# Edge values as three bf16 parts: a graph layer with its edge sums moved to bf16 matmuls

## The chip, the cores and the metric

The kernel runs on one core of a Trainium2 chip. A core has a matrix engine (TensorE, PE in the profile; PEld are its weight loads), a vector engine (VectorE, DVE), an engine for activation functions (ScalarE, ACT), GpSimd (POOL), which here issues the indirect DMAs, and SyncE (SP), which here issues nearly all other DMAs. Each engine works through its own instructions in the order in which the kernel gives them, and waits for another engine or a DMA where an instruction needs it. Matmuls write to PSUM, which this kernel divides into six banks named "mm" and two named "seg"; everything else lies in SBUF or in DRAM.

The metric is device time in microseconds, median over the runs of the kernel.

## The reference

One layer of a graph network on 6250 nodes of 256 features, with 106250 edges of 64 features. In short:

```python
xn = layernorm(x)
sums = segment_sum(edge_attr, src, n)                 # this is what the change touches
agg  = sums / maximum(segment_sum(ones, src, n), 1.0)
gnn  = relu(concat(xn, agg, u) @ W1 + b1) @ W2 + b2
mix  = 4 layers of: h = layernorm(x); x += linear_attention(h)
                    h = layernorm(x); x += gelu(h @ W1 + b1) @ W2 + b2
x = x + gnn + mix(xn)
x = x + relu(relu(z @ We1[e] + be1[e]) @ We2[e] + be2[e])   # z = layernorm(x), e = argmax(z @ router)
```

All is in fp32. The edge sums don't depend on the layers of `mix`; they are needed only after the last attention.

## The kernel before, in words

The nodes are worked on in 13 groups of 512 (the last has 106). X, the running sum of all nodes, stays in SBUF for the whole kernel. There are no queues that a planner fills: the order of the instructions is the order of the Python code, which is written out by hand (`manual_schedule`), and each engine keeps it.

**Layer 0's first half.** A loop over the groups normalizes x (`norms_a`, `norms_b`), transposes it (`norm1_t`), makes k and q of layer 0 (`qk`), transposes them (`context_t`) and adds to the attention's context (`context`).

**The layer loop.** For l = 0, 1, 2 and each group g, one iteration does the feed-forward part of layer l for group g and the attention's first half of layer l+1 for it: `ff_in` (eight outputs of 512 columns, each into an mm bank, L209, with a GELU on ACT to `hid`, L212), `attn_out_t` (transposes), `context_t(g-1)`, `ff_out` (L223), `norm1(g)`, `context(g-1)` (L499), `attn_out(g+2)` (L184), `norm1_t`, `qk` (L419 for k, L453 for q) and at its end `norm2(g+2)`. `norm2` takes statistics on DVE (L119, L120), a square root on ACT (L121, tile sd) and normalizes on DVE (L127). What `norm2` makes is used by `attn_out_t` of the next iteration; its square root stands on ACT ahead of the next iteration's GELUs.

**The edge work** is spread through both. An edge is a lane of one of 831 tiles of 128 edges; a batch is four tiles, and there are 208 batches. For a tile, a 128x128 matrix eq is 1 where two edges of the tile have the same source; eq times the tile's edge rows gives each edge the sum over all edges of the tile with its source. One edge per source then adds its row to a table in DRAM (`tabs`); the others are sent to a dump row, which the last of the 66 columns, a falling weight, decides. The steps of a batch:

- `edge_load`: two DMAs on SP, the edge values (128x4x64, fp32) and `all`, the sources of the batch, repeated on all 128 partitions (int32)
- `edge_match`: on DVE, eq from `all` and `srcf`, the sources as fp32, one per partition (L352)
- `edge_sum`: on PE, four fp32 matmuls of 66 columns into a seg bank (L365; each takes two passes in the profile), and a copy to `s` on ACT (L367)
- `edge_add`: on DVE the row numbers (L379, L381), then four indirect DMAs that add in DRAM (L383, POOL)

`edges(n)` does n times: an add, a sum, a load and a match, each of another batch; loads and matches run ahead of the sums, the adds one batch behind. In the layer loop `share` says how often each of the four calls of an iteration does this: (2, 1, 1, 2) in most iterations of l = 0 and 1. The calls stand after `ff_in`, after `norm1`, after `norm1_t` and after `qk`; the last stands just ahead of `norm2`.

**The rest** (from about 2100 us) is the last layer, the graph network's own part, the router and the experts; no edge work is in it but the reading of the tables.

## Time and profile before

| | |
|---|---|
| median of 3 runs | 2975.72 us (2973.36 to 2979.73) |
| the profiled execution: time, span | 2972.65 us, 2970.9 us |
| busy: PE, PEld, DVE | 2849.9, 2056.6, 1536.1 us |
| busy: ACT, POOL | 1126.9, 1458.1 us |
| mean granted clock of PE | 0.976 |
| layer 0's first half | about 40 to 205 us |
| layer loop, l = 0, 1, 2 | about 205 to 830, 840 to 1480, 1480 to 2100 us |

The profile gives for each engine its busy time, and a chain of waits, followed back from the last instruction, whose shares say which engine was waited for last. A group of instructions stands under its line, its engine and its tiles ("seg<-edge,eq"), with how many there are, their busy time in us, the mean duration in ns and the idle time of the engine just before them. The timeline lists instructions by start and duration in us, like ones in a row together, with the idle time before them in brackets and what ended it. In the windows view a line is a stretch: its length, then busy us (and instructions) of PE, PEld, DVE, ACT and POOL, the granted clock of PE, the DMA engines' share and GB/s.

### The profile page before, as it was taken

The page shows a single profiled execution, that of the slowest core. Times are in us where ns is not written, and L with a number is a line of the kernel's source. Part 1 is how long each engine was busy: PE and PEld are TensorE (multiplying, and loading weights), DVE is VectorE, ACT ScalarE, POOL GpSimd, SP SyncE. Part 2 cuts the span into 40 slices and gives each one's busy share as a digit, 9 for nine tenths or more (in the row PEclk, how much of TensorE's full clock was granted, in tenths as well). Part 3 has the DMA queues.
Part 4 walks back from the last instruction along what each step waited for, and adds up shares of the span by engine and source line. Part 5 has one row for each costly group of instructions (what it writes and reads, how often), then busy time and mean ns, then how long its engine had stood idle before and what let it go on. Part 6 is the DMA issues. An engine that isn't in the chain of part 4 may idle for free.

```text
span 2970.9 us, 36212 instructions
## 1 busy us (share of the span) xinstructions
PE 2849.9 (96%) x12594; PEld 2056.6 (69%) x12594; DVE 1536.1 (52%) x4194; ACT 1126.9 (38%) x1995; POOL 1458.1 (49%) x1108
## 2 busy tenths in 40 slices
PE   7989999999989999999899999999799999999977
PEld 5767777777766777777767777777566766765654
DVE  7874645555546464646455555544343543543453
ACT  6754343434334344343443434344223223223232
POOL 0445777777747777777746656454001001001057
PEclk9999999999989999999999999999899999999888
DMA  8234555655555555555734443231200101102152
GB/s 257 35 50 84 75 96 75 97 73 97 79 110 82 89 82 88 78 94 78 133 59 79 76 75 49 42 43 18 74 15 29 36 22 29 36 22 72 55 188 76
DMA packets 368983, 219.12 MB, mean 74 GB/s; under 512 B 265913, under 2 KB 333469, under 8 KB 368792
## 3 DMA queue, kind: packets, MB, share of 16 engines
q1 hardware_dynamic: 241832, 175.32, 22.9%
q0 software_dynamic: 126144, 40.61, 17.3%
q8 instruction: 102, 1.67, 0.2%
q14 instruction: 89, 0.73, 0.1%
q10 hardware_dynamic: 816, 0.79, 0.1%
HBM read 135.46 MB, written 85.49 MB: 74 GB/s over the span
## 4 chain that ended last, share of the span: by engine, by line
PE 87%; DVE 7%; ACT 2%; issue 2%; POOL 1%; DMA 1%; POOLq 0%; SPq 0%; ACTq 0%; DVEq 0%
PE mm L223 23%; PE mm L209 23%; PE seg L365 5%; PE mm L184 5%; PE mm L419 5%; PE mm L499 4%; PE mm L453 4%; PE mm L699 3%; PE mm L135 3%; PE mm L715 3%; PE mm L700 2%; PE mm L487 1%; PE mm L479 1%; POOL out_x L987 1%; PE mm L972 1%
## 5 line engine op out<-in xcount | busy, mean ns | idle before, releaser
L383 POOL DMA_INDIRECT tab<-s,row x831 | 1313.5, 1581 | 738.4 <-issue 352.8
L209 PE MATMUL mm<-hT,w 128*128 128x512 f32 (+1 forms) x1664 | 686.5, 570 | 5.8 <-ACT hid L212 4.0
L223 PE MATMUL mm<-w,hid 128*128 128x256 f32 (+1 forms) x3136 | 687.8, 380 | 0.0
L223 PEld LDWEIGHTS mm<-w,hid 128*128 128x128 f32 (+1 forms) x3136 | 592.5, 190 | 80.1
L209 PEld LDWEIGHTS mm<-hT,w 128*128 128x128 f32 x1664 | 301.3, 190 | 354.7 <-issue 321.9
L121 ACT ACTIVATE sd<-mv,eps 128x4 f32<-128x4 f32 (+1 forms) x117 | 34.8, 297 | 991.3 <-DVE mv L120 991.1
L225 DVE TENSOR_TENSOR X<-mm,X 128x512 f32<-128x512 f32 (+1 forms) x100 | 68.1, 681 | 632.1 <-PE mm L223 632.1
L775 POOL DMA_INDIRECT xtab<-rows,to x49 | 48.2, 984 | 643.1 <-DVE to L773 574.1
L212 ACT ACTIVATE hid<-mm,col 128x512 f32<-128x512 f32 (+1 forms) x416 | 249.1, 669 | 101.1 <-PE mm L209 98.8
L365 PEld LDWEIGHTS seg<-edge,eq 128*128 128x128 f32 x1662 | 207.2, 192 | 21.5 <-issue 17.2
L365 PE MATMUL seg<-edge,eq 128*128 128x66 f32 x1662 | 202.7, 270 | 0.0
L139 ACT ACTIVATE hT<-mm,col 128x512 f32<-128x512 f32 (+1 forms) x208 | 145.0, 748 | 142.1 <-PE mm L135 140.8
L184 PE MATMUL mm<-M,qT 128*128 128x256 f32 (+1 forms) x784 | 191.3, 400 | 2.3 <-DVE M L539 2.3
L419 PE MATMUL mm<-hT,wqkv 128*128 128x512 f32 (+1 forms) x416 | 183.5, 584 | 3.5 <-ACT hT L139 3.5
L499 PE MATMUL mm<-z,kt 128*128 128x256 f32 (+1 forms) x784 | 181.8, 385 | 0.2 <-ACT kt L481 0.2
L453 PE MATMUL mm<-wqkv,hT 128*128 128x256 f32 (+1 forms) x784 | 177.7, 379 | 0.0
L453 PEld LDWEIGHTS mm<-wqkv,hT 128*128 128x128 f32 (+1 forms) x784 | 148.4, 190 | 40.7 <-issue 22.5
L184 PEld LDWEIGHTS mm<-M,qT 128*128 128x128 f32 (+1 forms) x784 | 156.2, 201 | 27.4 <-DVE M L539 4.2
L499 PEld LDWEIGHTS mm<-z,kt 128*128 128x128 f32 (+1 forms) x784 | 147.4, 192 | 19.1 <-ACT kt L481 0.4
L135 PE MATMUL mm<-ident,z 128*128 128x128 f32 x882 | 124.8, 277 | 28.3 <-DVE z L127 16.9
L352 DVE TENSOR_TENSOR eq<-all,srcf 128x512 f32<-128x512 int32 x208 | 142.9, 687 | 3.1 <-DMA all<-in_srct 2.7
L379 DVE TENSOR_SCALAR a<-s,twice,dump 128x4 f32<-128x4 f32 x208 | 60.4, 291 | 154.4 <-ACT s L367 154.4
(209 smaller groups left out, 3310.5 us busy)
## 6 DMA issues: line engine op xcount, KB each, us to landing
all<-in_srct SPq DMA_DIRECT2D x207, 256.0 KB, 3.8
xtab<-zero SPq DMA_DIRECT2D x32, 1036.0 KB, 10.2
edge<-in_edge SPq DMA_DIRECT2D x207, 128.0 KB, 2.7
tab<-s,row POOLq DMA_INDIRECT x831, 3.3
xg<-xtab SPq DMA_DIRECT2D x32, 259.0 KB, 5.9
w<-in_w SPq DMA_DIRECT2D x8, 1024.0 KB, 13.8
tab<-zero SPq DMA_DIRECT2D x40, 162.5 KB, 4.9
tb<-tab SPq DMA_DIRECT2D x48, 130.0 KB, 4.1
```

The source lines that it names most:

```text
L135: nc.tensor.transpose(ps[:, j * P:j * P + r], z[j][:r, k * P:(k + 1) * P], ident[:r, :r])
L139: nc.scalar.activation(hT[:, k, :cnt], ps[:, :cnt], AF.Identity, bias=col[:, bcol + k:bcol + k + 1], scale=col[:, gcol + k:gcol + k + 1])
L184: nc.tensor.matmul(ps[:r, j, :], qT[:, k, c0:c0 + r], M[:, k, :], start=(k == 0), stop=(k == 1))
L209: nc.tensor.matmul(ps[:, :cnt], w[:, k, b * P:(b + 1) * P], h[:, k, :cnt], start=(k == 0), stop=(k == 1))
L212: nc.scalar.activation(hid[:, :cnt], ps[:, :cnt], AF.Gelu, bias=col[:, c:c + 1], scale=1.0)
L223: nc.tensor.matmul(ps[:r, j, :], hid[b][:, c0:c0 + r], w[:, b, :], start=(b == 0), stop=(b == NHB - 1))
L352: nc.vector.tensor_tensor(out=eq[:, :m], in0=ALL.pop(b)[:, :m], in1=srcf[:, t0:t0 + m].unsqueeze(2).to_broadcast([P, m, P]), op=ALU.is_equal)
L365: nc.tensor.matmul(ps[:, i, :], eq[:, i, :], e[:, i, :], start=True, stop=True)
L383: nc.gpsimd.indirect_dma_start(out=tabs[i], out_offset=bass.IndirectOffsetOnAxis(ap=row[:, i:i + 1], axis=0), in_=s[:, i, :DE + 1], in_off ...
L419: nc.tensor.matmul(ps[:, :cnt], w[:, k, c:c + P], h[:, k, :cnt], start=(k == 0), stop=(k == 1))
L453: nc.tensor.matmul(ps[:r, j * D:(j + 1) * D], h[:, k, (j0 + j) * P:(j0 + j) * P + r], w[:, k, :D], start=(k == 0), stop=(k == 1))
L499: nc.tensor.matmul(ps[:, b, :], kt[b][:r, j * P:(j + 1) * P], z[:r, j, :], start=(j == 0), stop=(j == n - 1))
```

## The change

Each edge value is split into three bf16 numbers whose sum is exactly the fp32 value: the upper half of its 32 bits is a bf16 by itself (`upper`, a view of the same memory that takes every second half-word), the rest is a subtraction on DVE, the upper half of the rest is the second part, and what is still left, another subtraction, is the third. eq becomes bf16, which holds 0 and 1 exactly. The sum of a tile is then three bf16 matmuls into the same PSUM columns in place of one in fp32. The new step `edge_split` makes the parts, as far ahead as `edge_match` makes eq.

The sources that `all` repeats are now 16 bits wide. They are loaded once into an unused part of qT (`wide`), cast on DVE (`half`), written to DRAM (`near`) and loaded from there.

The edge work of layer 0's first half is taken out: groups 2 to 12 there had one `edges()` each, and group 1 two matches. Now group 2 has the cast and the write to DRAM, group 10 two loads, group 11 two matches and splits and a load. `share` in the layer loop is (2, 1, 1, 2) also for the first four groups of l = 2, and (2, 1, 1, 1) for the later ones, where it was (2, 1, 1, 1) for the first six and (1, 1, 1, 1) then.

```diff
+    near = dram.tile([P, ET], I16, name="near")
...
+            wide = qT[:, 1, N - ET:].bitcast(I32)
+            half = qT[:, 1, N - 2 * ET:N - ET].bitcast(I16)[:, :ET]
+            nc.sync.dma_start(out=wide, in_=srct.rearrange("o (p t) -> (o p) t", p=P))
+            near_row = near.rearrange("(o p) t -> o (p t)", o=1)
...
-                al = ep.tile([P, CB * EB, P], I32, name="all", bufs=2)
+                al = ep.tile([P, CB * EB, P], I16, name="all", bufs=2)
                 nc.sync.dma_start(out=al[:, :m].rearrange("p m e -> p (m e)"),
-                                  in_=srct[:, t0 * P:(t0 + m) * P].to_broadcast([P, m * P]))
+                                  in_=near_row[:, t0 * P:(t0 + m) * P].to_broadcast([P, m * P]))
...
-                eq = ep.tile([P, EB, P], F32, name="eq", bufs=3)
+                eq = ep.tile([P, EB, P], BF16, name="eq", bufs=3)
...
+            def upper(t):
+                return t.bitcast(BF16).rearrange("p j (c h) -> p j c h", h=2)[:, :, :, 1]
+
+            def edge_split():
+                b = steps["split"]
+                if b >= steps["load"]:
+                    return
+                steps["split"] += 1
+                m = min(EB, ET - b * EB)
+                e = EDGE[b]
+                rest = ep.tile([P, EB, DE], F32, name="rest", bufs=3)
+                nc.vector.tensor_tensor(out=rest[:, :m], in0=e[:, :m, :DE], in1=upper(e[:, :m, :DE]), op=ALU.subtract)
+                low = ep.tile([P, EB, DE], BF16, name="low", bufs=3)
+                nc.vector.tensor_tensor(out=low[:, :m], in0=rest[:, :m], in1=upper(rest[:, :m]), op=ALU.subtract)
+                PART[b] = upper(rest), low
...
-                e = EDGE.pop(b)
+                e = upper(EDGE.pop(b))
+                mid, low = PART.pop(b)
...
-                    nc.tensor.matmul(ps[:, i, :], eq[:, i, :], e[:, i, :], start=True, stop=True)
+                    nc.tensor.matmul(ps[:, i, :], eq[:, i, :], e[:, i, :], start=True, stop=False, skip_group_check=True)
+                    nc.tensor.matmul(ps[:, i, :DE], eq[:, i, :], mid[:, i, :], start=False, stop=False, skip_group_check=True)
+                    nc.tensor.matmul(ps[:, i, :DE], eq[:, i, :], low[:, i, :], start=False, stop=True, skip_group_check=True)
...
                     edge_match()
+                    edge_split()
...
             norm1_t(0, 0)
-            edge_load()
-            edge_load()
             clear_tabs()
...
-                if g == 1:
+                if g == 2:
+                    nc.vector.tensor_copy(half, wide)
+                    nc.sync.dma_start(out=near, in_=half)
+                elif g == NG - 3:
+                    edge_load()
+                    edge_load()
+                elif g == NG - 2:
                     edge_match()
+                    edge_split()
                     edge_load()
                     edge_match()
-                elif g:
-                    edges()
+                    edge_split()
...
-                    share = ((1, 0, 0, 1) if g + 1 == NG else (2, 1, 1, 1) if g + 2 == NG or (l + 2 == DEPTH and g < 6)
-                             else (2, 1, 1, 2) if l + 2 < DEPTH else (1, 1, 1, 1))
+                    share = ((1, 0, 0, 1) if g + 1 == NG else (2, 1, 1, 1) if g + 2 == NG or (l + 2 == DEPTH and g > 3)
+                             else (2, 1, 1, 2))
```

More of the change, by code (lines that the diff above doesn't have):

```diff
@@ L12 @@
 I32 = mybir.dt.int32
+I16 = mybir.dt.int16
 BF16 = mybir.dt.bfloat16
@@ L321, in clear @@
                                   in_=zero[:, :XROW].unsqueeze(1).to_broadcast([P, XCLEAR // P, XROW]))
-            EDGE, ALL, EQ, SUM = {}, {}, {}, {}
-            steps = {"load": 0, "match": 0, "sum": 0, "add": 0}
+            EDGE, ALL, EQ, SUM, PART = {}, {}, {}, {}, {}
+            steps = {"load": 0, "match": 0, "split": 0, "sum": 0, "add": 0}
             def edge_load():
@@ L354, in edge_match @@
                 EQ[b] = (eq, m)
+            def upper(t):
[12 more added lines that the diff above has]
+                PART[b] = upper(rest), low
             def edge_sum():
                 b = steps["sum"]
-                if b >= steps["match"]:
+                if b >= min(steps["match"], steps["split"]):
                     return
```

## The prediction

> **What bounds it now.** I read the page first: busy shares, then the chain that ended last, then the costliest groups.

> ```profile
> PE 2849.9 (96%) x12594; PEld 2056.6 (69%) x12594; DVE 1536.1 (52%) x4194; ACT 1126.9 (38%) x1995; POOL 1458.1 (49%) x1108
> PE 87%; DVE 7%; ACT 2%; issue 2%; POOL 1%; DMA 1%; POOLq 0%; SPq 0%; ACTq 0%; DVEq 0%
> L365 PE MATMUL seg<-edge,eq 128*128 128x66 f32 x1662 | 202.7, 270 | 0.0
> L352 DVE TENSOR_TENSOR eq<-all,srcf 128x512 f32<-128x512 int32 x208 | 142.9, 687 | 3.1 <-DMA all<-in_srct 2.7
> ```

> PE sets the end, and the edge sums (L365) are on it, so their cost looks like gain. But the chain names only what came last; I asked next how near the second thing comes. The timeline of one steady iteration of the layer loop (six batches; 50.15 us from one L209 start to the next), PE:

> ```profile
> 465.89 1.90 PE L365 MATMUL seg<-edge,eq 128*128 128x66 f32 x16
> 467.63 13.96 PE L209 MATMUL mm<-hT,w 128*128 128x512 f32 x32
> 481.43 1.90 PE L365 MATMUL seg<-edge,eq 128*128 128x66 f32 x16
> 483.16 1.04 PE L135 MATMUL mm<-ident,z 128*128 128x128 f32 x8
> ```

> The same timeline, DVE and then ACT:

> ```profile
> 471.28 0.28 DVE L379 TENSOR_SCALAR a<-s,twice,dump 128x4 f32<-128x4 f32 x1
> 471.60 0.16 DVE L381 TENSOR_TENSOR row<-srcf,a 128x4 int32<-128x4 f32 x1
> 471.68 0.68 DVE L352 TENSOR_TENSOR eq<-all,srcf 128x512 f32<-128x512 int32 x1
> ...
> 473.29 0.42 DVE L119 BATCH_NORM_STATS2 st<-X 128x6 f32<-128x256 f32 x1
> ```

> ```profile
> 475.54 0.30 ACT L121 ACTIVATE sd<-mv,eps 128x4 f32<-128x4 f32 x1 [4.88 <-DVE mv L120]
> 475.85 1.28 ACT L212 ACT_TABLE_LOAD   x1
> 477.15 4.16 ACT L212 ACTIVATE hid<-mm,col 128x512 f32<-128x512 f32 x7
> ```

> The reader is to see one queue. At the iteration's end DVE does two batches of edge work (471.28 to 473.29, 1.0 us each), then norm2's statistics; ACT waits for these 4.88 us with sd, and the GELUs of the ff_in that PE began at 467.63 stand behind sd. ff_in makes eight outputs, but six banks ("mm") exist: output 7 needs the bank of GELU 1. PE gets to it at 467.63 + 10.35 = 477.98 (matmul 25 of 32 at 0.43 us); GELU 1 ends at 477.84. The cover is 0.15 us. So PE bounds this loop, with DVE and then ACT 0.15 us behind.

> [...] 512 elements take 0.69 us, 260 (L671) 0.43. [...] the new eq keeps fp32 srcf as an input, so I leave it at 0.69. [...] in the bf16 matmuls of the router (timeline, PE):

> ```profile
> 2228.91 0.25 PE L764 MATMUL mm<-oh,ones 128*128 128x96 bf16 x3
> 2229.01 0.25 PE L767 MATMUL mm<-oh,ones 128*128 128x32 bf16 x4
> 2229.12 0.68 PE L209 MATMUL mm<-hT,w 128*128 128x512 f32 x1
> ```

> Seven matmuls, each with its own weights, in 0.21 us. [...] stretches with the granted clock:

> ```profile
> 829.20:832.60 3.40, 1.99 (x14) 1.57 (x12) 2.06 (x9) 1.98 (x10) 2.70 (x2) 1.00 1.35 134
> 832.90:849.60 16.70, 12.28 (x33) 8.92 (x34) 5.24 (x14) 2.73 (x5) 12.39 (x8) 0.50 0.84 187
> ```

> The idle there before L487 was 2.27 us; one of 1.57 us (2073.96) brought no half clock.

> **The change, part by part.** *Sums on PE.* Before, a lone batch takes 251.10 to 251.94 = 0.84 us, a pair 465.89 to 467.63 = 1.74. After, 12 bf16 matmuls of 64 or 66 columns. Bounds for one: 25 ns (32 columns above) and 57 ns for the two that read every second half-word, were they paced like the fp32 pass (66/256 of the 216 ns of L223, and its 2 ns). I take 29, since 96, 64 and 32 columns together took 100 ns. The next fp32 weight load costs 0.11. Lone: 11 x 0.029 + 0.11 = 0.43; pair 0.79 (slow end 0.65 and 1.22). All 208 batches: 85 us of PE work gone.

> *Splits on DVE.* Two dependent subtractions of 256 elements: 0.43 + 0.04 to the dependent one (as L225 to L226, 0.73 for 0.69), then 0.34 to the next instruction (0.60 for 512): 0.81 us a batch, 168 us in all. An optimistic end is 0.4 (half), a pessimistic one 0.9.

> *The steady iteration.* From the end of ff_out to norm2, DVE now has four splits more (edges calls 2, 3, and two in 4). Two lie before qk's max, where DVE had 0.34 + 1.02 us of waits for PE: 1.62 minus these, and with PE there 0.7 earlier but DVE now last, leaves the second max 0.1 late. Two lie in the last call: +1.62 bare. So sd and GELU 1 are 1.7 late. PE meanwhile saves 0.7 before qk and 0.95 on the pair before ff_in, and waits for them: output 7 starts 0.155 after GELU 1 (as where GELU 1 was late, at 1255), an idle of 1.7 + 0.7 + 0.95 = 3.35 us. Of all PE savings only the pair after ff_in (0.95) is left on the path. Net 1.72 - 0.95 = +0.77 us.

> *The clock.* [...] mean +1.1 per iteration.

> *By layer.* Groups 0 to 10 are stalled: l=0 and l=1: 11 x 1.87; groups 11 and 12 have no norm2 behind them and keep PE's gain, 3.0: +17.6 each. l=2: four groups with six batches, 52.0 against 49.25 = +11.1; seven with one batch in the last call, idle 1.9, no half clock: 49.1 against 49.25 (two) and 48.4 (five): +3.2; last two groups -3.0: +11.3. Sum +46.5.

> *Layer 0's first half.* DVE bounds it (13.2 of 15 us busy): a, row, eq at 1.0 us leave groups 3 to 10: -8.0. In group 1 two eq and the wait for DMA all (1.6) go: -2.8. Group 2 gets the cast for the eq: L293, of the same length, took 0.56. Group 11 gets two eq and two splits, under PE's work at the end (181 to 205), where three sums leave: -1. Sum -11.5.

> *Waits.* The sums on PE wait for low too; it is made two batches ahead, as eq is, so PE finds it done. *DMA.* all halves in bytes; near (0.2 MB out) and wide (0.4 MB in) are two issues on SP. Behind near's wait on SP only the edge loads of group 10 stand, some 90 us later; the two early edge loads leave the busy first 40 us. The loads keep their lead, as SP waits for the sums (L333, 1099 us) and runs ahead of DVE. Nothing: covered by 8 us between calls; uncovered, a late load costs its 3.8 us.

> *POOL.* 24 adds at 1.86 us = 44.6 us an iteration, some lengthened to 2.0 under an eq; with splits 46 to 50. Hidden under 50.9; it would cap the gain if PE ran at 47.4.

> Sum: 46.5 - 11.5 = +35; the profiled execution took 2972.65 (span 2970.9), so 3008, and 3 us more against the median 2975.72: 3010.

> **Rivals.** (1) The stall comes, the clock stays: +0.77 per iteration; 5.5 + 5.5 + 6.9 - 11.5 = +6, 2982. For it: long idles in the trace all lie among short matmuls. Against: the half clocks. (2) The other side: splits cheaper than the cover. Place: DVE between the second max and norm2's statistics. With 0.4 us a split, max 2 is on PE's time again and GELU 1 only 0.1 late: -0.85 an iteration, 2930; without any delay the PE gain shows, -87 - 11.5: 2877. It decides below 0.62 us a split. [...] (3) Dearer: strided reads at the fp32 pace leave 0.52 for 0.95 on the pair, +14 over the loops; splits of 0.9 add 10: 3025 to 3040. For: these reads are in no row of before.

> **How the numbers follow.** Forecast 0.52 (2997 to 3026), rival 1 0.19, rival 2 0.17, rival 3 0.12. The time is the forecast's. 2968 to 3036 leaves out rival 2 and the end of rival 3. A measurement of this kernel can tell about 0.2% (2969.8 to 2981.7) from no change: half of rival 1 lies in it, 0.10; faster 0.18, slower 0.72.

> **What would show it.** Right: sums of 0.4 us a batch; PE waiting for ACT hid at the seventh output of ff_in, about 3.3 us in some 26 groups and 1.9 in seven, DVE without a gap from ff_out's end to sd; iterations of 50.9, or 52 with half clock; first half 11 us shorter. Wrong: iterations of 47.5 without that wait; splits under 0.6 us; waits for DMA or POOL in their place.

## The result: 1.7% slower, and where the time went

The changed kernel takes 3028.24 us (median of 4 runs, 3023.29 to 3029.56), the kernel before, beside it, 2977.72 us (2973.36 to 2981.24). The ratio is 1.0167, with a 95% interval of 1.0148 to 1.0186. The profiled execution has a span of 3027.8 us, 56.9 more than before.

The stages lie between the first matmuls of ff_in (L209 before, L211 after) of the layers. In us, from the two traces:

| stage | before | after | difference | predicted |
|---|---|---|---|---|
| up to the layer loop | 220.8 | 222.0 | +1.2 | -11.5 |
| l = 0 | 637.0 | 655.0 | +18.0 | +17.6 |
| l = 1 | 637.8 | 655.6 | +17.8 | +17.6 |
| l = 2 | 625.5 | 642.9 | +17.3 | +11.3 |
| the rest | 849.8 | 852.4 | +2.7 | 0 |

First the page of the changed kernel and its groups of instructions (busy us, mean ns, then the idle time ahead of them and its cause):

```profile
PE 2806.6 (93%) x13425; PEld 1970.1 (65%) x13425; DVE 1695.9 (56%) x4611; ACT 1119.8 (37%) x1995; POOL 1466.6 (48%) x1108
L211 PE MATMUL mm<-hT,w 128*128 128x512 f32 (+1 forms) x1664 | 718.2, 587 | 97.5 <-ACT hid L214 95.7 <-ACT hT L141 1.7
L359 DVE TENSOR_TENSOR eq<-all,srcf 128x512 bf16<-128x512 int16 x208 | 142.9, 687 | 0.3 <-issue 0.3
L376 DVE TENSOR_TENSOR rest<-edge 128x256 f32<-128x256 f32 x208 | 87.0, 418 | 0.0
L378 DVE TENSOR_TENSOR low<-rest 128x256 bf16<-128x256 f32 x208 | 88.3, 425 | 7.1
```

PE is busy 43 us less (226 us of the span run at half clock, for 145 before, which stretches what is left) and DVE 160 us more. What PE no longer works it waits: ff_in's matmuls wait 95.7 us for the GELUs, where they waited 4.0. The chain of waits of this page breaks off after 0% of the span and can't be read; the timeline takes its place. One steady iteration (51.05 us, or more where the clock is halved), on PE, DVE and ACT:

```profile
474.67 10.54 PE L211 MATMUL mm<-hT,w 128*128 128x512 f32 x24
488.45 6.52 PE L211 MATMUL mm<-hT,w 128*128 128x512 f32 x8 [3.23 <-ACT hid L214]
```

```profile
480.41 0.69 DVE L359 TENSOR_TENSOR eq<-all,srcf 128x512 bf16<-128x512 int16 x1
481.01 0.42 DVE L376 TENSOR_TENSOR rest<-edge 128x256 f32<-128x256 f32 x1
481.47 0.42 DVE L378 TENSOR_TENSOR low<-rest 128x256 bf16<-128x256 f32 x1
481.81 0.52 DVE L407 TENSOR_SCALAR a<-s,twice,dump 128x4 f32<-128x4 f32 x1
...
483.85 0.42 DVE L121 BATCH_NORM_STATS2 st<-X 128x6 f32<-128x256 f32 x1
```

```profile
486.10 0.30 ACT L123 ACTIVATE sd<-mv,eps 128x4 f32<-128x4 f32 x1 [6.70 <-DVE mv L122]
486.41 1.28 ACT L214 ACT_TABLE_LOAD   x1
487.71 3.58 ACT L214 ACTIVATE hid<-mm,col 128x512 f32<-128x512 f32 x6
```

Read from the bottom: GELU 1 starts 13.04 us after ff_in (before: 477.15 - 467.63 = 9.52), because sd comes 11.43 us after it (before 7.91), because norm2's statistics do, and ahead of these stand two batches of edge work that now take 2 us each. PE stops after 24 of 32 matmuls. In the windows view (length; busy us of PE, PEld, DVE, ACT, POOL; granted clock) the first line is this iteration, with half clock behind the wait (mean granted clock 0.94), the second one without (1.00):

```profile
474.67:528.54 53.87, 50.57 (x263) 35.56 (x259) 31.69 (x84) 19.94 (x35) 38.53 (x25) 0.94 0.46 65
632.16:683.21 51.05, 47.74 (x263) 34.47 (x259) 32.04 (x84) 19.83 (x35) 38.20 (x25) 1.00 0.50 68
```

### The profile page after: what moved, and what is told of

It reads as the page before. It is cut to its first block, busy times and chain, and to the rows that moved or that the text cites. A ratio compares the mean times of both kernels' runs of the same rounds, so it can differ in the third digit from the quotient of the medians.

```text
span 3027.8 us, 38235 instructions
## 1 busy us (share of the span) xinstructions
PE 2806.6 (93%) x13425; PEld 1970.1 (65%) x13425; DVE 1695.9 (56%) x4611; ACT 1119.8 (37%) x1995; POOL 1466.6 (48%) x1108
## 5 line engine op out<-in xcount | busy, mean ns | idle before, releaser
L211 PE MATMUL mm<-hT,w 128*128 128x512 f32 (+1 forms) x1664 | 718.2, 587 | 97.5 <-ACT hid L214 95.7
L225 PE MATMUL mm<-w,hid 128*128 128x256 f32 (+1 forms) x3136 | 687.7, 380 | 0.0
L225 PEld LDWEIGHTS mm<-w,hid 128*128 128x128 f32 (+1 forms) x3136 | 592.3, 190 | 80.0
L211 PEld LDWEIGHTS mm<-hT,w 128*128 128x128 f32 x1664 | 309.0, 195 | 468.7 <-issue 321.3
L186 PE MATMUL mm<-M,qT 128*128 128x256 f32 (+1 forms) x784 | 197.9, 410 | 2.4 <-DVE M L568 2.4
L407 DVE TENSOR_SCALAR a<-s,twice,dump 128x4 f32<-128x4 f32 x208 | 70.0, 336 | 155.1 <-ACT s L395 155.1
L359 DVE TENSOR_TENSOR eq<-all,srcf 128x512 bf16<-128x512 int16 x208 | 142.9, 687 | 0.3 <-issue 0.3
L137 PEld LDWEIGHTS mm<-ident,z 128*128 128x128 f32 x882 | 101.5, 141 | 56.2 <-issue 26.1
L121 DVE BATCH_NORM_STATS2 st<-X 128x6 f32<-128x256 f32 (+1 forms) x343 | 137.4, 401 | 0.1
```

What stands on the lines that cost most here:

```text
L121: nc.vector.bn_stats(out=st[:r, j, :], in_=source(j))
L137: nc.tensor.transpose(ps[:, j * P:j * P + r], z[j][:r, k * P:(k + 1) * P], ident[:r, :r])
L186: nc.tensor.matmul(ps[:r, j, :], qT[:, k, c0:c0 + r], M[:, k, :], start=(k == 0), stop=(k == 1))
L211: nc.tensor.matmul(ps[:, :cnt], w[:, k, b * P:(b + 1) * P], h[:, k, :cnt], start=(k == 0), stop=(k == 1))
L225: nc.tensor.matmul(ps[:r, j, :], hid[b][:, c0:c0 + r], w[:, b, :], start=(b == 0), stop=(b == NHB - 1))
L359: nc.vector.tensor_tensor(out=eq[:, :m], in0=ALL.pop(b)[:, :m], in1=srcf[:, t0:t0 + m].unsqueeze(2).to_broadcast([P, m, P]), op=ALU.is_equal)
```

## The experiments

The theory to test is the prediction's: the splits stand on DVE ahead of norm2's statistics, so the square root and the GELUs come late, and PE's saving turns into a wait before output 7 of ff_in. The rivals: the time is lost on PE itself (the reads of every second half-word, the banks), on GpSimd or the DMAs, or by the new distribution of the batches. All ratios below are to the kernel before, run on the same chip.

### The parts of the change, one at a time

**Splits alone** (`before_splits`): the kernel before, plus `upper` and

```diff
...
                 EQ[b] = (eq, m)
+                e, al = EDGE[b], ALL.pop(b)
+                rest = al[:, :m, :DE].bitcast(F32)
+                low = al[:, :m, DE:DE + DE // 2].bitcast(BF16)
+                nc.vector.tensor_tensor(out=rest, in0=e[:, :m, :DE], in1=upper(e[:, :m, :DE]), op=ALU.subtract)
+                nc.vector.tensor_tensor(out=low, in0=rest, in1=upper(rest), op=ALU.subtract)
```

> The kernel before (fp32 sums, int32 sources, edge work in the first half) with the two subtractions of edge_split behind each match; nothing reads their results, which go into the part of all that the match has used up. Theory: DVE alone makes GELU 1 1.6 to 1.7 us late, and PE, which comes no earlier, waits that long before output 7: 51.8 us in iterations of six batches (22 of them, +37), nothing in those of l = 2, whose last call has one batch, and +0.85 in each of ten groups of the first half: about 3020 us (3008 to 3035). Rival (the time is lost by the sums on PE or by their operands, not by DVE): 2975 to 2985 us.

Measured: 3079.55 us, ratio 1.0337 (1.0320 to 1.0354). The layers take 677.0, 677.9 and 639.7 us (+40, +40, +14), the first part 234.5 (+13.7).

**bf16 sums without the splits** (`no_splits`): the changed kernel with

```diff
-                rest = ep.tile([P, EB, DE], F32, name="rest", bufs=3)
-                nc.vector.tensor_tensor(out=rest[:, :m], in0=e[:, :m, :DE], in1=upper(e[:, :m, :DE]), op=ALU.subtract)
...
-                PART[b] = upper(rest), low
+                PART[b] = upper(e[:, :, :DE]), upper(e[:, :, :DE])
```

> The changed kernel without the two subtractions: the second and third matmul of a tile read the upper halves again (mid and low parts are left out of the sums). PE's work is that of the changed kernel, DVE's is less by 168 us. Theory: GELU 1 is 1.7 us earlier, but PE still comes to ff_in 0.95 us earlier than before, so a wait of about 0.95 us stays before output 7: 48.4 us in iterations of six batches, 46.5 to 47 in those of five; 2905 to 2935 us. Rival PE: 51 us and 3020 us. Rival POOL: 50 us and 2990 us.

Measured: 2934.38 us, ratio 0.9846 (0.9829 to 0.9862); layers 621.3, 623.7 and 618.7 us (-15.7, -14.1, -6.9).

**The distribution alone** (`before_sched`): the kernel before with the loop over groups and the `share` of the change; the two loads ahead of `clear_tabs` leave too.

```diff
-                if g == 1:
+                if g == NG - 3:
+                    edge_load()
+                    edge_load()
+                elif g == NG - 2:
                     edge_match()
                     edge_load()
                     edge_match()
-                elif g:
-                    edges()
...
-                    share = ((1, 0, 0, 1) if g + 1 == NG else (2, 1, 1, 1) if g + 2 == NG or (l + 2 == DEPTH and g < 6)
-                             else (2, 1, 1, 2) if l + 2 < DEPTH else (1, 1, 1, 1))
+                    share = ((1, 0, 0, 1) if g + 1 == NG else (2, 1, 1, 1) if g + 2 == NG or (l + 2 == DEPTH and g > 3)
+                             else (2, 1, 1, 2))
```

> The kernel before with the changed kernel's distribution of the batches alone: no edge work in groups 1 to 10 and 12 of layer 0's first half (two loads in group 10, two matches and a load in group 11), and the changed kernel's shares in l = 2; fp32 sums, int32 sources, no splits. Theory as the trace of the changed kernel corrects it (groups there took 14.78 us for 15.13, as DVE then waits for ACT): the first half 3 to 5 us shorter; l = 2 8 to 10 us longer, since its first four iterations take 50.15 for 49.25 and the others 49.25 for 48.4: 2976 to 2984 us. By the prediction's own step: the first half 10 us shorter, 2970 to 2977 us.

Measured: 2980.21 us, ratio 0.9993 (0.9982 to 1.0003). The first part takes 220.1 us (-0.7), l = 2 637.9 us (+12.3).

The timelines of PE in the same kind of iteration, with splits alone and without them:

```profile
551.37 10.52 PE L209 MATMUL mm<-hT,w 128*128 128x512 f32 x24
564.00 5.40 PE L209 MATMUL mm<-hT,w 128*128 128x512 f32 x8 [2.12 <-ACT hid L212]
```

```profile
652.24 10.54 PE L211 MATMUL mm<-hT,w 128*128 128x512 f32 x24
663.63 3.70 PE L211 MATMUL mm<-hT,w 128*128 128x512 f32 x8 [0.85 <-ACT hid L214]
```

What follows. DVE's two subtractions make the wait without any change on PE, and with the bf16 matmuls alone, all of whose reads of the edge values are strided, the kernel is faster than before: the rival PE falls. (The 16-bit sources were not run alone; eq takes 687 ns with them and without.) The effects add up in an iteration: the splits bring 2.1 us of wait, the earlier PE 0.9, together 3.0 of the 3.2 seen in the changed kernel.

The expectation for the splits was 60 us too low, in several places. First, the wait is 0.4 us longer: GELU 1 comes 2.37 us later than before, of which 1.62 are the two batches' splits, as expected; 0.24 is `a` of the second batch, which takes 0.52 us there too; 0.23 is that in this kernel the subtractions write where eq reads and start 0.72 us after it, not 0.60; and 0.28 is that qk's maximum comes later. Second, eight of ten such waits in l = 0 were followed by half clock (ff_in then takes 17.8 us or more instead of 16.3), which the expectation had left out. Third, l = 2 was to lose nothing, but most of its iterations wait 0.8 us too, and it takes 14 us more; and the first part lost 13.7 us for 8.5.

The distribution alone can't be told from no change. In its trace l = 2 is 12.3 us longer: PE work moved there, and 3.2 us more in its last iteration, which has more half clock. How much the first half gives back, the traces don't say closely, since that stage took 220.8, 227.2 and 222.1 us in three executions of the same code (before, `before_late`, and `before_match_late` below). In the ten traces without the edge work it took 218.9 to 222.0.

### The order on DVE

**The whole fourth call behind norm2**, in the changed kernel (`late`) and in the kernel before (`before_late`), same edit:

```diff
                     qk(l + 1, g)
-                    edges(share[3])
                     if g + 2 < NG:
                         norm2(g + 2)
+                    edges(share[3])
```

> The changed kernel with one statement moved: the last of the four calls of the edge work stands behind norm2 of group g+2, not ahead of it. Same instructions, same counts. Theory (the splits delay norm2's statistics, so the square root and the GELUs, so the bank of output 7): the wait before output 7, 3.2 us, is gone, iterations take 47.2 to 47.6 us instead of 51.04 to 54.4, the half clock behind the waits goes too; 26 groups times 3.6 to 4.5 us: 2885 to 2920 us in all. Rival POOL (24 adds of 1.9 us are what bounds an iteration): 49 to 50 us an iteration, 2970 to 2995 us. Rival PE (the waits come from the reads or the banks, not from DVE's order): 51 us as now, 3020 to 3030 us.

> The kernel before with the same statement moved. Theory: there is only the cover of 0.15 us to add to, PE bounds the loop either way: 50.1 us an iteration, 2970 to 2981 us. Rival (the order is worth something by itself, whatever the sums cost): under 2950 us.

Measured: `late` 3217.82 us, ratio 1.0797 (1.0776 to 1.0817); `before_late` 3084.12 us, ratio 1.0354 (1.0315 to 1.0393). Both far outside every range I had given. PE, ACT and POOL of `late`, one iteration:

```profile
511.36 10.54 PE L211 MATMUL mm<-hT,w 128*128 128x512 f32 x24
522.15 3.70 PE L211 MATMUL mm<-hT,w 128*128 128x512 f32 x8 [0.25 <-ACT hid L214]
...
539.25 6.22 PE L225 MATMUL mm<-w,hid 128*128 128x256 f32 x14 [10.01 <-ACT hT L141]
```

```profile
526.48 0.37 ACT L395 COPY s<-seg 128x264 f32<-128x264 f32 x1
538.14 0.38 ACT L395 COPY s<-seg 128x264 f32<-128x264 f32 x1 [11.29 <-DMA tab<-s,row]
538.41 1.45 ACT L141 ACTIVATE hT<-mm,col 128x512 f32<-128x512 f32 x2
```

```profile
522.00 1.63 POOL L411 DMA_INDIRECT tab<-s,row  x1 [5.41 <-issue]
```

The reader is to see two things. The wait before output 7 is all but gone (0.25 us), as the theory said. And three times as much has come up in another place: the second copy to s after ff_in waits 11.29 us for an add to land. (All such waits of `late` come to 278 us, of `before_late` to 107, of the kernel before to 1.) There are four buffers for s, so a batch's copy needs the adds of the batch four earlier to have landed, and these are the first of the fourth call, which start at 522.00 only, behind norm2. In l = 2 of `before_late`, where every fourth call has a single batch, so that the copy needs an older add, nothing changed: 625.4 us for 625.5. Behind the copy on ACT stands hT, which ff_out needs. The place of the fourth call ahead of norm2 thus had a purpose that neither the diff nor the page of before shows: its adds keep the four buffers turning.

**Only the splits of the fourth call behind norm2** (`splits_late`), **or loads, matches and splits** (`match_late`), adds and sums ahead of it in both:

```diff
-                    edges(share[3])
+                    for _ in range(share[3]):
+                        edges_out()
                     if g + 2 < NG:
                         norm2(g + 2)
+                    for _ in range(share[3]):
+                        edges_in()
```

This is `match_late`; `edges_out` is an add and a sum, `edges_in` a load, a match and a split. In `splits_late` the loads and matches stay ahead as well.

> The changed kernel with only the splits of the fourth call (two batches, 1.6 us of DVE) moved behind norm2; its adds, sums, loads and matches stay ahead of it. Theory (the wait before output 7 is what DVE does ahead of norm2's statistics): the wait shrinks from 3.2 us to about what the kernel without splits showed, 0.9 to 1.5 us, since the splits of the second and third call are still there; 48.6 to 49.4 us an iteration of six batches, no half clock behind it, 2935 to 2960 us in all. Rival (moving edge work behind norm2 costs by itself, as in the run with the whole call moved): over 3050 us.

> The changed kernel with loads, matches and splits of the fourth call behind norm2; its adds and sums stay ahead of it. Theory: GELU 1 comes another 1.4 us earlier, PE waits for nothing before output 7 and its gain shows: 47.3 to 47.9 us an iteration, 2890 to 2920 us in all. It also tells what made the run with the whole call moved slow: if the adds (which then reach the DMA engines together with the loads, so that the copies to the four s buffers wait for them), this run doesn't have that wait; if the late loads or matches, it has it: ACT waits of several us for the adds at L395's copy and over 3000 us.

Measured: `splits_late` 2958.39 us, ratio 0.9919 (0.9900 to 0.9938), 49.1 to 49.6 us an iteration and a wait of about 1.5 us, but for the first stalled one of each layer (51.7 us, with a wait of 2.2 us and the half clock that was not expected); `match_late` 2946.63 us, ratio 0.9889 (0.9864 to 0.9914). So moving 1.6 us of DVE work past norm2 turns the change from 1.7% slower to 0.8% faster: the step of the prediction that its sign rests on is shown. `match_late` fell short of its range by 27 us. It has no waits of 10 us, but some of up to 5.7 us at the copy to s, of the same kind as `late`: PE waited 15.7 us in all for hT before ff_out, ACT 38.4 us for adds at the copy. And PE still waited 20.1 us in all before output 7, where the expectation had none.

### The four buffers, and what is left

`late_s5` is `late` with five buffers, `ml_s5` is `match_late` with five:

```diff
-                s = ep.tile([P, EB, DE + 2], F32, name="s", bufs=4)
+                s = ep.tile([P, EB, DE + 2], F32, name="s", bufs=5)
```

`ml_s5_qk` also has the third call's load, match and split inside qk:

```diff
-                    edges(share[2])
-                    qk(l + 1, g)
+                    for _ in range(share[2]):
+                        edges_out()
+                    qk(l + 1, g, share[2])
...
                     ek.append(t)
+                for _ in range(inner):
+                    edges_in()
                 if g:
                     nc.vector.tensor_tensor(out=ctxt["l"], in0=ctxt["l"], in1=alpha, op=ALU.mult)
```

> The kernel in which the whole fourth call stands behind norm2, now with five buffers for s instead of four. Theory (that run was slow because the second copy to s after ff_in reuses the buffer of the first add of the fourth call, which is then only just under way; ACT waits some 10 us there, and hT and ff_out behind it): with a fifth buffer that copy needs the add of the third call, long done, and the wait is gone: 47.5 to 48.5 us an iteration, 2895 to 2925 us. Rival (GpSimd or the DMA engines can't do the adds in time whatever the buffers): the wait moves to a later copy, 3050 us or more.

> The run with loads, matches and splits of the fourth call behind norm2 (adds and sums ahead of it), with five buffers for s. Theory: what was left there, 16 us of PE waiting for hT before ff_out and the half clock behind three of these waits, goes; the 20 us before output 7 stay: 2922 to 2934 us. Rival (these waits have another cause): 2943 to 2950 us.

> As the run before, and load, match and split of the third call stand inside qk, where DVE waits 0.2 and 1.2 us for ACT, not ahead of qk's maximum. Theory: the maximum comes 0.4 to 0.8 us earlier, the 1.5 us of match and split cover most of a wait that is there anyway, so GELU 1 is 0.5 to 1.2 us earlier and the 20 us before output 7 go too: 2902 to 2920 us. Rival (the end of DVE's chain before norm2 doesn't move, since the work only changes sides): as the run before within 5 us.

Measured: `late_s5` 2917.69 us, ratio 0.9783 (0.9767 to 0.9799); `ml_s5` 2923.95, 0.9812 (0.9796 to 0.9828); `ml_s5_qk` 2911.11, 0.9761 (0.9745 to 0.9777). All three within their ranges. The copy to s (groups of instructions) in `late`, then in `late_s5`:

```profile
L395 ACT COPY s<-seg 128x264 f32<-128x264 f32 x208 | 74.7, 377 | 278.8 <-DMA tab<-s,row 277.9 <-ACT sd L123 0.4 <-PE seg L393 0.3
```

```profile
L395 ACT COPY s<-seg 128x264 f32<-128x264 f32 x208 | 72.8, 378 | 8.0 <-DMA tab<-s,row 5.6 <-PE mm L508 1.1 <-PE seg L393 0.6
```

One buffer of 1 KB a partition takes 9% of the time away: 278 us of waiting become 8. GpSimd has the same 831 adds in both, so it was not too slow for them. In `ml_s5_qk`, DVE does match and split where it had waited for ACT, and ff_in runs through:

```profile
500.88 0.23 DVE L469 TENSOR_SCALAR nb<-mx 128x2 f32<-128x2 f32 x1
500.94 0.69 DVE L359 TENSOR_TENSOR eq<-all,srcf 128x512 bf16<-128x512 int16 x1
501.55 0.42 DVE L376 TENSOR_TENSOR rest<-edge 128x256 f32<-128x256 f32 x1
502.00 0.43 DVE L378 TENSOR_TENSOR low<-rest 128x256 bf16<-128x256 f32 x1
502.34 0.15 DVE L480 TENSOR_TENSOR l<-l,alpha 128x2 f32<-128x2 f32 x1
```

```profile
503.86 13.98 PE L211 MATMUL mm<-hT,w 128*128 128x512 f32 x32
```

Its steady iteration is 47.55 us, 2.6 less than before, and its layers take 617.1, 614.5 and 611.8 us. This is the version that beats both kernels, by 2.4% and, by the two ratios to before (0.9761 and 1.0167), by 4.0%.

**The kernel before in that order** (`before_match_late`) asks whether the order is worth something without the change. Its edit is that of `match_late` in the kernel before (there is no split to move), with four buffers.

> The kernel before with loads and matches of the fourth call behind norm2, its adds and sums ahead of it: the order that made the changed kernel faster, with fp32 sums. Theory: PE bounds the loop before and has nothing to gain from an earlier GELU 1: 50.1 to 50.2 us an iteration, 2972 to 2985 us; a few iterations may wait for hT as the changed kernel with this order did, since GpSimd and the four s buffers are the same. Rival (this order is worth its 1 to 2% by itself, and the change nothing): 2930 to 2955 us.

Measured: 2998.01 us beside 3000.76 us on that chip, ratio 0.9990 (0.9982 to 0.9998). ACT of an iteration whose ff_in began at 619.26:

```profile
627.59 3.58 ACT L212 ACTIVATE hid<-mm,col 128x512 f32<-128x512 f32 x6
```

GELU 1 starts 8.33 us after ff_in, 1.2 us earlier than before, and the iteration takes 50.15 us, as before to the hundredth. PE bounded the kernel before, so slack behind it buys nothing; and of what PE saves, only a part comes through without the slack (`no_splits`: 1.4 us an iteration, where `ml_s5_qk` has 2.6). With this order and the change the gain on the kernel before is 1.1% (`match_late`), with this order alone 0.1%. The kernel before with a fifth buffer and with the work inside qk was not run; that these alone buy nothing there is argued, from a PE that has no wait in these iterations.

### The end of layer 0's first half

`half_fix` spreads what the change put into group 11:

```diff
-                elif g == NG - 3:
+                elif g == NG - 4:
                     edge_load()
                     edge_load()
-                elif g == NG - 2:
+                elif g == NG - 3:
                     edge_match()
                     edge_split()
+                elif g == NG - 2:
                     edge_load()
                     edge_match()
+                elif g == NG - 1:
                     edge_split()
```

> The changed kernel with the two matches and splits that stood in group 11 of the first half spread over groups 10, 11 and 12 (loads in group 9). Theory: group 12's step is back near 11.5 us, the half clock from 200 to 214 us doesn't come, and the layer loop starts at 218 to 219.5 us instead of 222.0; the rest as in the changed kernel: 3022 to 3028 us. Rival (the half clock and the idle there come from the end of the first half itself): the loop starts at 221 us or later.

Measured: 3024.19 us, ratio 1.0144 (1.0127 to 1.0161); the loop starts at 220.7 us. The half clock still comes, for 10.24 us at 202.69; only PE's wait of 1.56 us ahead of it (at 197.21 in the changed kernel) is gone. The loop's start lies between what the theory asked for (219.5 at most) and the rival's 221. The seven traces with the changed kernel's first half have it at 221.3 to 222.0, so spreading the two matches and splits gained 0.6 to 1.4 us, and the rival holds for the larger part. The half clock lies where PE runs context_out's few short matmuls. It is there in all ten traces without edge work in the first half, and in two of the four with it; before, with idles of the same lengths there, didn't have it. What decides it was not shown. In the steps of 3.413 us in which the granted clock changes (last section), the array's work, by an estimate, fell to 0.38 at 204.67 in before, with full clock behind it, and to 0.31 at 197.21 in the changed kernel, with half clock behind it.

## Why the prediction was right, and where not

The sign and the mechanism of the loop held; 3028 lies 18 us above the forecast of 3010, inside the range (2968 to 3036) but just outside the likeliest case's own (2997 to 3026). From trace to trace it was +56.9 us for +35: of the 22 that are missing, 12.7 are layer 0's first half, 6.0 are l = 2, and 2.7 the rest, whose cause is open. That l = 0 and l = 1 are right to 0.4 us is in part luck, as shown below. Step by step:

- **The queue behind ff_in** (DVE to norm2's statistics to sd to GELU 1, a cover of 0.15 us): right. `splits_late` moves the change to the other side of 1 by taking 1.6 us out of it, `before_match_late` shows that the cover itself was not what bounded the kernel before.
- **Sums on PE**: right. The matmuls start 28 to 35 ns apart (30 in the middle, estimate 29), a pair took 0.72 us (estimate 0.79; its own terms give 0.78). Against the pace of 57 ns that rival 3 needs for the reads of every second half-word, it has no ground.
- **Splits on DVE**: right. 0.42 us each, 0.80 a batch for 0.81. Rival 2 needed less than 0.62.
- **The steady iteration**: 51.04 us for 50.92, a wait of 3.23 us for 3.35 (3.43, counted as there from where matmul 25 would have started); 1.55 for 1.9 in l = 2's iterations with one batch in the last call. The 0.12 more come from one instruction: `a` of the second batch (L407) takes 0.52 us instead of 0.28 in these iterations. In the one at 372.83, where it took 0.30, the wait was 3.00 and the iteration 50.81. Why it is longer behind a split, is open; the same 0.52 was there with splits alone.
- **The clock**: that half clock follows some of these waits was right; how often it does, and what it costs, were wrong. The 1.1 us an iteration were my estimate, which no view of before showed. In the traces of before and after the granted clock changes only in steps of 3.413 us (last section). In the changed kernel's full groups, steps with 2.12 us of this wait or more were followed by half clock, and those with 1.97 or less weren't; in group 12, whose matmuls have 106 columns, waits of 1.57 to 1.63 us were followed by it in all three layers. Of the idle of 2.27 us that the prediction names, the stretch at full clock that it shows holds only 1.4 (PE 1.99 of 3.40 busy), among short matmuls. Of the 24 waits of more than 3 us, ten were followed by half clock; of each pair of these, the first had 6.83 us of it behind it and cost 2.8 to 3.5 us (in the first pair of a layer about 0.5 of it is a longer wait), the second had 3.41 and cost 1.4 to 1.5. In l = 0 that is 9.1 us for the 12 that 11 times 1.1 make. An iteration of 51.04 us is 14.95 steps, so the wait moves only 0.16 us a time against them, lies divided between two of them for several iterations, and then falls mostly into one, twice in a row.
- **By layer**: the sums of l = 0 and 1 are right by luck, as two errors cancel. Their ten steady intervals cost +18.2 us in l = 0. The first interval gained 2.2 us, which I had counted among the stalled. The last two were to gain 3.0 and lost 2.0: ff_in of group 11 still stands behind norm2 of group 12 and waits 1.41 us, and the next iteration got 3.41 us of half clock. In l = 2 the same error shows, since there is less against it: intervals of six batches +11.7 (predicted 11.1), of five +3.4 (3.2), the first -1.3, the last two +3.5 instead of -3.0.
- **Layer 0's first half**: this step failed: -11.5 predicted (the parts that it lists come to -11.8), +1.2 measured (and -5 at most, against the longest of the three traces of the same code above). The groups have become shorter by 0.35 us, not by 1.0. The view that shows why is DVE's timeline, before and then after:

```profile
140.40 0.17 DVE L279 RECIPROCAL rs<-v 128x4 f32<-128x4 f32 x1
```

```profile
135.06 1.37 DVE L278 TENSOR_SCALAR X<-X,mv,rs 128x256 f32<-128x256 f32 x4
137.13 0.18 DVE L281 RECIPROCAL rs<-v 128x4 f32<-128x4 f32 x1 [0.69 <-ACT v L276]
```

DVE waits 0.69 us for ACT where it waited for nothing before. I had read "13.2 of 15 us busy" as DVE being the bound, and took its work off one for one. The bound is a chain that goes from DVE to ACT and back, and the edge work had stood inside a wait. The 4 us that were gained by group 12 went at its end: the stretch from its k to the layer loop takes 30.4 us for 25.2, with 13.65 us of half clock. `before_sched` has it too, without any split: 220.1 us.

- **DMA and POOL hidden**: right for the changed kernel, where the copies to s wait 0.6 us in all; but by a margin that the prediction did not see, so that this was luck too. It argued from POOL's 46 to 50 us an iteration, while the limit was when an add has landed, and how many s buffers there are until then.
- **The rivals**: without half clock behind the waits (9.1, 9.4 and 4.9 us in the three layers) the kernel would have taken some 3005 us (an estimate), not rival 1's 2982, which needs the first half's gain and that of the last two groups. The full PE gain (2877) came in no run: without the splits, PE still waits 0.85 us for GELU 1, and the best order reached 2911.

## What to carry to other kernels

Work taken off the bounding engine is sure to pay only up to the distance to the next chain, so measure that distance before you price the saving; here it was 0.15 us. Beyond it, the saving pays only where the next chain runs through the same engine too (1.4 of 2.6 us here); the whole of it came when that chain was shortened by moving work behind the thing that others wait for. Before you move a step, list what its instructions hand back (here, buffers for a copy on a third engine) as well as what they delay: the same move made the changed kernel 6% slower with four buffers and 4% faster with five. An engine that is busy 88% of a loop need not be its bound alone: its waits can be part of a chain through another engine.
